# Three tables of places remade: the same 8,797 steps of a graph network kernel in another order of issue

## The chip, the cores and the metric

The kernel runs on one core of a Trainium2 chip. Its metric is device microseconds (us) for one launch. The kernel before took 1741.71 us in the median of three runs (1741.22 to 1742.57).

Five engines work on their own queues, each strictly in the order in which the program issued to it: TensorE (PE, matmuls and transposes), VectorE (DVE), ScalarE (ACT), GpSimd (POOL) and SyncE (SP, which here only issues DMAs). An instruction that needs another engine's result waits at the head of its own queue, and all that stands behind it waits too.

## What is computed

Sixteen independent graphs of 1024 nodes with 256 features go through two layers. `adj` holds 0 or 1 here, so of the first layer's four edge kinds only the first occurs.

```python
# layer 0: gate every edge by the nodes' own product
e     = leaky(einsum('bid,bjd->bij', x * a0, x))         # slope 0.2
alpha = sigmoid(where(adj == 1, e, -max))
x     = layernorm(x + einsum('bij,bjd->bid', alpha, x) + bias)
# layer 1: attention with four heads of 64 features
Wh    = (x @ W).reshape(B, N, H, F)
e     = leaky_relu(e_src[:, :, None, :] + e_dst[:, None, :, :], 0.2)
alpha = softmax(where(A > 0, e, -1e9), axis=2)
Hout  = elu(einsum('bijh,bjhf->bihf', alpha, Wh))
x     = layernorm(x + Hout.reshape(B, N, H * F))
```

The softmax is not evaluated edge by edge. Each exponential is a product of a factor of the source and one of the target, with one of two slopes. So the kernel only decides for each edge which slope holds (`pos`, a 0/1 matrix), multiplies that matrix by the targets' factors (`acc`), multiplies the whole mask by the same factors (`total`), and joins the two sums afterwards.

## The kernel before, in words

`stages` (line 194) writes one graph's work as some fifty Python generators, one for each stage. Every `yield` ends a **step**: one instruction, or a few of one kind. `issue` (line 1229) decides the order in which all steps of all graphs are issued. It takes a table of **places** for each graph: `FIRST` (line 1008) for graph 0, `LAST` (line 1120) for graph 15, `TIMES` (line 902) for those between. A table has a number for each step of each stage; graph b's numbers are shifted by b times `PERIOD` (112.0), everything is sorted by number, and the steps are issued in that order. Equal numbers keep the order of the table. The numbers are written like microseconds, but nothing waits for a clock: only the order counts, and no scheduler changes it afterwards (`manual_schedule`). Semaphores hold each instruction until its inputs are there, whatever the order.

Three graphs are always under way at once, so the queue of each engine is a weave of three graphs' stages. In the order of one graph, with the engine and the line of its instruction:

- loads of `adj` (aload, SP, L267) and of x (xload, SP, L253); `cast` to bf16 (ACT, L276); `turn`, a transpose of the mask by DMA (SP, L291; in graph 0 on PE, L286); `mask` (ACT, L298).
- `xt`, `xtc`, `xta`: x transposed and scaled (PE L319, ACT L330, ACT L344).
- `score` (PE, L356, 12 steps), `leak` (ACT, L368) and `leaky` (DVE, L376), `sigmoid` (ACT, L382). Only the upper triangle is computed; `below` (PE, L395) and `lower` (DVE, L401) mirror it, `upper` (DVE, L412) masks it, `self_loop` (DVE, L419) adds the identity.
- `agg` (PE, L427, 16 steps), then `residual` (DVE, L459), `moments0` and `gathered0` (DVE, L444 and L450), `spread0` (POOL, L468 and L469), `shift0` (DVE, L477), `norm0` (ACT, L489): the first layer's end.
- `yt`, `ytc`, `project`, `wh` (PE L498, ACT L507, PE L517, ACT L529). `sources`, `rows`, `keep_rows` (ACT L535, PE L541, ACT L552 and a DMA at L553) put one row per head and block into DRAM; `sload` (SP, L648) reads a row back, spread over all partitions.
- `top_dve` (DVE, from L560) and `top_pe` (PE, L588 and L591), `exps` (ACT, L598): the factors. `product` (DVE, L619; half of them on ACT, L614, in graph 15), `high` (ACT, L633) and `low` (DVE, L640) split them into two parts in `gm`, of which there is one buffer for all graphs.
- `pos` (DVE, L658, 64 steps) and `acc` (PE, L670, 64 steps of four matmuls): for each half of the nodes and each head, eight steps. `acc_low` (ACT, L685) and `acc_sum` (DVE, L693) empty the sums. There are six `pos` buffers and two accumulators.
- `all_edges` (ACT, L705, 16 steps) and `total` (PE, L713, 32 steps of four matmuls), `total_kept`, `total_less`.
- `weigh`, `divide`, `elu`, `join` (DVE L780, L772, L790 to L810; ACT L816; in graphs 14 and 15 the wide products go to ACT, L767), `moments1`, `gathered1`, `spread1`, `shift1`, `norm1`, and `leave` (SP, L876) sends a half of the graph out. `weigh_end` to `join_end` work on the last head of graph 15 alone.

Four PSUM banks (`ps_t`) are shared by `xt`, `score`, `below`, `agg`, `yt`, `project`, `rows`, `top_pe` and `total`: the next of these waits until the fourth before it has been read. The order of issue so also sets the order in which the banks go round, and what a bank waits for.

Of the kernel before, what the change touches and what calls it, by code (L numbers as in the profile page):

```python
# [193 lines left out]
def stages(nc, k, pl, b, xg, adjg, outg, sums, span, zinv):  # L194
# [675 lines left out]
    def leave():  # L870
# [32 lines left out]
    "xload": [-190.36],  # L903
    "aload": [-141.21, -134.94, -129.14, -126.41, -107.72, -95.92, -52.91, -49.35],
    "cast": [-133.33, -126.54, -110.85, -106.42, -72.33, -55.28, -40.89, -29.41],
    "turn": [-133.00, -118.97, -108.09, -86.35, -62.89, -45.14, -38.49, -26.07],
    "mask": [-126.25, -118.09, -94.06, -70.56, -52.12, -40.03, -32.69, -25.15],
    "setup": [-54.43, -50.76, -47.38],
    "xt": [-69.63, -66.83, -65.59, -61.38],
    "xtc": [-65.35, -64.69, -63.96, -57.76],  # L910
    "xta": [-60.02, -56.47, -53.23, -47.62, -40.80, -39.84, -35.73, -22.45],
    "score": [
        -55.95, -54.26, -52.86, -52.85, -50.30, -47.61, -41.77, -41.05, -37.61, -36.60,
        -31.53, -19.69,
    ],
    "leak": [
        -54.25, -52.28, -52.05, -51.99, -45.24, -41.19, -38.48, -36.59, -34.23, -28.07,
        -26.47, -19.19,
    ],
    "leaky": [  # L920
        -53.92, -51.61, -45.43, -45.41, -41.52, -40.38, -37.19, -36.20, -32.91, -26.88,
        -25.80, -17.05,
    ],
    "sigmoid": [-50.37, -36.56, -28.45, -23.28, -23.17, -15.81, -5.09, 4.38],
    "below": [-43.48, -40.73, -36.17, -28.75, -25.55, -24.80, -21.22, -11.11, 7.22, 7.95],
    "lower": [-41.97, -37.35, -33.23, -27.18, -24.41, -23.38, -19.01, -9.26, 8.37, 17.62],
    "upper": [-24.74, -21.21, -20.88, -18.06, 1.37, 12.57, 17.16, 22.61],
    "self_loop": [-22.52, -20.95, -18.10, -17.88, 3.26, 14.07, 18.13, 24.49],
    "agg": [
        -18.25, -16.27, -15.06, -15.02, -4.11, -4.03, -2.54, 0.32, 5.09, 8.13, 15.85,  # L930
        17.47, 21.46, 23.59, 23.78, 24.56,
    ],
    "residual": [-8.35, -7.46, -1.27, 2.37, 22.46, 22.48, 26.43, 27.74],
    "moments0": [-5.49, -4.53, 5.61, 8.01, 23.75, 25.11, 27.16, 28.13],
    "gathered0": [4.13, 6.42, 7.91, 10.51, 26.40, 27.32, 28.51, 29.05],
    "spread0": [13.40, 31.26],
    "shift0": [17.29, 31.54],
    "norm0": [21.66, 21.89, 22.47, 23.38, 34.53, 34.91, 35.50, 35.54],
    "yt": [27.46, 27.57, 36.68, 36.99],
    "ytc": [29.00, 29.33, 39.29, 39.57],  # L940
    "project": [32.52, 32.60, 33.90, 39.19, 40.28, 40.33, 40.41, 40.81],
    "wh": [33.22, 36.59, 37.58, 40.10, 40.68, 42.17, 42.34, 43.12],
    "sources": [41.16, 45.78],
    "rows": [41.83, 54.07],
    "keep_rows": [44.82, 56.53],
    "top_dve": [43.38, 45.01, 45.39, 50.81, 51.81],
    "top_pe": [44.42, 46.92],
    "exps": [51.81],
    "product": [53.02, 53.37, 53.98, 54.66, 58.34, 66.43, 69.20, 72.08],
    "high": [53.76, 54.40, 58.33, 58.56, 61.32, 68.49, 71.81, 73.63],  # L950
    "low": [54.19, 57.97, 61.74, 62.89, 71.04, 72.63, 75.29, 76.96],
    "sload": [50.80, 79.07, 83.92, 88.62, 102.34, 116.17, 128.36, 142.07],
    "pos": [
        57.31, 58.08, 60.13, 63.67, 69.85, 70.05, 71.57, 77.68, 80.69, 81.39, 82.09,
        82.79, 83.51, 84.84, 85.08, 85.50, 94.75, 97.25, 97.29, 97.48, 99.31, 100.22,
        100.86, 101.86, 104.39, 105.08, 105.66, 107.42, 108.55, 108.94, 109.06, 109.44,
        111.06, 112.18, 112.18, 112.50, 114.43, 114.99, 117.57, 118.23, 118.61, 122.99,
        125.51, 126.22, 128.00, 128.98, 130.58, 132.32, 133.80, 134.68, 135.40, 135.59,
        136.35, 141.70, 144.45, 144.66, 145.90, 146.60, 148.13, 149.39, 151.16, 153.05,
        156.93, 159.83,  # L960
    ],
    "acc": [
        66.06, 67.27, 68.14, 69.24, 71.32, 72.44, 73.71, 78.80, 83.16, 83.97, 84.72,
        85.39, 85.74, 87.50, 88.94, 90.52, 99.28, 99.52, 100.60, 101.24, 101.47, 101.85,
        102.15, 102.38, 108.43, 108.66, 109.45, 109.46, 109.72, 110.12, 110.70, 110.77,
        114.66, 115.11, 115.34, 116.25, 116.73, 118.20, 118.35, 119.33, 130.24, 130.46,
        130.54, 131.53, 132.09, 132.57, 134.85, 134.91, 141.46, 142.49, 142.93, 144.35,
        145.14, 145.81, 145.91, 146.87, 153.97, 154.83, 159.23, 159.59, 164.73, 165.20,
        165.32, 166.33,
    ],  # L970
    "acc_low": [
        79.49, 79.83, 96.76, 97.23, 103.47, 104.76, 112.24, 112.31, 122.02, 122.21,
        134.93, 135.59, 149.34, 149.98, 169.77, 170.85,
    ],
    "acc_sum": [
        80.66, 80.96, 97.10, 98.04, 105.15, 105.96, 112.53, 112.54, 127.47, 127.48,
        136.59, 136.70, 149.39, 150.00, 171.97, 175.58,
    ],
    "all_edges": [
        24.35, 76.79, 79.33, 79.88, 81.06, 82.66, 85.63, 89.08, 96.83, 101.38, 102.99,  # L980
        108.02, 111.52, 113.15, 116.96, 118.15,
    ],
    "total": [
        77.14, 77.24, 78.75, 79.22, 79.40, 79.41, 79.97, 80.39, 84.60, 84.83, 85.08,
        85.73, 89.40, 89.80, 90.91, 93.34, 97.93, 100.95, 101.71, 106.58, 107.02, 107.21,
        109.68, 110.76, 112.06, 113.36, 114.66, 114.68, 117.04, 118.18, 118.28, 119.92,
    ],
    "total_kept": [80.79, 83.22, 90.91, 93.71],
    "total_less": [112.64, 113.12, 119.31, 124.40],
    "weigh": [119.49, 129.29, 190.71, 191.25, 196.08, 212.23],  # L990
    "divide": [
        125.16, 126.39, 127.60, 129.50, 130.49, 134.23, 134.70, 134.85, 200.68, 201.14,
        206.69, 213.74, 214.56, 214.57, 216.22, 218.60,
    ],
    "elu": [133.27, 142.72, 214.93, 220.17],
    "join": [136.57, 142.87, 142.93, 145.63, 220.24, 222.78, 225.82, 228.23],
    "moments1": [146.58, 148.42, 152.65, 153.15, 223.48, 227.82, 229.78, 230.58],
    "gathered1": [146.81, 150.62, 154.63, 154.74, 228.81, 229.65, 230.64, 230.81],
    "spread1": [164.98, 232.04],
    "shift1": [165.77, 237.22],  # L1000
    "norm1": [195.74, 197.90, 202.92, 203.03, 238.05, 240.07, 240.16, 240.29],
    "leave": [206.44, 240.93],
    "weigh_end": [222.86, 228.40],
    "divide_end": [222.94, 223.01, 223.09, 223.17, 228.57, 228.75, 228.92, 229.09],
    "elu_end": [223.25, 229.26],
    "join_end": [223.32, 223.40, 229.44, 229.61],
}
FIRST = {
    "aload": [-146.50, -146.40, -145.60, -145.40, -145.20, -144.50],
    "cast": [-146.00, -145.00, -144.10, -143.30, -142.40, -141.30, -140.80, -140.10],  # L1010
    "turn": [-145.50, -144.80, -144.00, -143.00, -141.90, -140.90, -140.30, -139.30],
    "mask": [-145.10, -144.30, -142.70, -142.60, -141.20, -140.50, -139.70, -139.00],
    "setup": [-145.90, -142.90, -140.70],
    "xt": [-147.40, -147.20, -146.90, -146.80],
    "xtc": [-147.10, -146.70, -146.30, -146.10],
    "xta": [-146.60, -145.70, -144.70, -143.40, -141.50, -140.90, -139.60, -138.50],
    "score": [
        -146.20, -144.90, -144.40, -143.70, -143.10, -142.30, -142.00, -141.80, -140.40,
        -139.10, -138.80, -137.70,
    ],  # L1020
    "leak": [
        -145.80, -144.60, -143.90, -143.50, -142.80, -142.20, -141.40, -140.60, -140.00,
        -138.40, -138.10, -137.30,
    ],
    "leaky": [
        -145.30, -144.20, -143.60, -143.20, -142.50, -141.70, -141.00, -140.20, -139.40,
        -138.30, -137.60, -137.20,
    ],
    "sigmoid": [-143.80, -142.10, -138.70, -137.80, -136.80, -136.70, -135.00, -134.80],
    "below": [  # L1030
        -141.60, -140.00, -139.80, -139.30, -138.20, -137.10, -136.90, -136.60, -135.50,
        -134.60,
    ],
    "lower": [
        -141.10, -139.90, -139.50, -139.20, -137.00, -136.50, -136.40, -135.70, -134.90,
        -132.90,
    ],
    "upper": [-138.90, -138.00, -136.30, -136.10, -135.20, -134.30, -134.20, -133.50],
    "self_loop": [-138.60, -137.50, -135.90, -135.40, -134.40, -133.30, -133.10, -131.70],
    "agg": [  # L1040
        -137.90, -137.40, -136.20, -136.00, -135.80, -135.30, -134.50, -133.80, -133.60,
        -133.20, -133.00, -132.50, -132.20, -132.10, -131.90, -131.00,
    ],
# [434 lines left out]
```

## Time and profile before

| what | value |
|---|---|
| median of three runs | 1741.71 us |
| span of the profiled execution, first to last instruction | 1739.6 us |
| mean granted TensorE clock | 0.990 |
| busy: PE, DVE, ACT, POOL | 97%, 94%, 71%, 6% |
| first steady stretch to last: PE busy from 200 to 1600 us | 1399.4 of 1400 us |
| PE busy, 0 to 80 us and 1650 to 1740 us | 69.7 of 80 us and 54.7 of 90 us |
| DVE busy, 0 to 80 us and 1650 to 1740 us | 35.8 of 80 us and 80.3 of 90 us |
| time from one graph to the next in the steady stretch | 104.44 us |

The profiled execution's span ends some 2.1 us short of the runs' median; the rest lies ahead of its first instruction and behind its last one. A busy share counts the time in which an engine has at least one instruction under way. Matmuls overlap: a matmul of `agg` is shown as 379 ns long, but the next one starts 216 ns after it. So a busy share of PE says that PE had something under way, and what a row costs is read from start to start.

### The profile page before, as it was taken

The numbers are of one execution on the slowest core, as the hardware profiler recorded it, in microseconds if no ns is written. First come the engines' busy times: TensorE is split into PE (matmuls) and PEld (weight loads), VectorE is DVE, ScalarE is ACT, GpSimd is POOL, SyncE is SP. The second block draws the span as 40 slices with busy tenths as digits, with TensorE's granted clock in tenths as the row PEclk, the third lists the DMA queues.
The fourth block names the chain that finished last, engine by engine and source line by source line (L and its number), as shares of the span: only waits on it lengthen the run. The fifth ranks groups of instructions, "written<-read, shape, count | busy, mean of one in ns | idle before, by whom it ended". The sixth has DMA issues, their size and how long they took to land.

```text
span 1739.6 us, 29647 instructions
## 1 busy us (share of the span) xinstructions
PE 1692.1 (97%) x10580; PEld 1492.5 (86%) x10580; DVE 1639.6 (94%) x3663; ACT 1239.4 (71%) x2766; POOL 106.8 (6%) x138
## 2 busy tenths in 40 slices
PE   8999999999999999999999999999999999999984
PEld 5789898998979889898998979889898898979883
DVE  5498999999999999999999999999999999999998
ACT  7674957759587685967759587685967859586784
POOL 0000000010000101000010000101000010000100
PEclk9999999999999999999999999999999999999987
DMA  5542333434334343333435334443343424422020
GB/s 190 129 116 67 98 98 92 110 92 131 88 89 101 105 125 92 94 101 92 109 92 129 91 86 102 105 128 91 89 107 92 110 67 117 105 71 55 26 68 26
DMA packets 249005, 168.59 MB, mean 97 GB/s; under 512 B 133010, under 2 KB 232468, under 8 KB 248852
## 3 DMA queue, kind: packets, MB, share of 16 engines
q1 hardware_dynamic: 248848, 166.63, 36.1%
q8 instruction: 86, 1.41, 0.3%
q14 instruction: 67, 0.55, 0.1%
q10 hardware_dynamic: 4, 0.00, 0.0%
HBM read 118.10 MB, written 17.04 MB: 78 GB/s over the span
## 4 chain that ended last, share of the span: by engine, by line
PE 91%; DVE 3%; ACT 2%; DMA 1%; issue 1%; POOL 0%; SPq 0%; ACTq 0%; DVEq 0%; POOLq 0%
PE acc L670 27%; PE agg L427 24%; PE tot L713 14%; PE e L356 13%; PE pw L517 7%; PE pg L395 3%; PE pt L498 2%; PE pt L319 1%; DVE pos L658 1%; DMA sbc<-sdram 1%; ACT prod L614 0%; DMA aT<-a 0%; PE pbc L591 0%; ACT gm L633 0%; ACT y L489 0%
## 5 line engine op out<-in xcount | busy, mean ns | idle before, releaser
L658 DVE SCALAR_TENSOR_TENSOR pos<-sbc,nd,mT 128x512 fp32r<-128x512 f32 x1024 | 737.4, 745 | 10.5 <-PE acc L670 5.0
L670 PE MATMUL acc<-gm,pos 128*128 128x260 f32 x4096 | 608.6, 292 | 8.9 <-DVE gm L640 5.0
L670 PEld LDWEIGHTS acc<-gm,pos 128*128 128x128 f32 x4096 | 536.8, 190 | 19.8 <-issue 5.7
L427 PE MATMUL agg<-xb,gate 128*128 128x256 f32 x2048 | 463.5, 379 | 0.2
L427 PEld LDWEIGHTS agg<-xb,gate 128*128 128x128 f32 x2048 | 379.9, 190 | 47.6 <-DVE gate L419 1.2
L713 PE MATMUL tot<-gm,allm 128*128 128x264 f32 x2048 | 328.8, 297 | 5.4 <-ACT gm L633 4.9
L713 PEld LDWEIGHTS tot<-gm,allm 128*128 128x128 f32 x2048 | 281.4, 189 | 9.7 <-ACT gm L633 5.1
L356 PE MATMUL e<-xT,xTa 128*128 128x512 f32 (+3 forms) x768 | 264.3, 489 | 2.2 <-ACT xTa L344 1.4
L356 PEld LDWEIGHTS e<-xT,xTa 128*128 128x128 f32 x768 | 135.1, 191 | 106.4 <-issue 55.3
L685 ACT COPY low<-acc 128x260 f32<-128x260 f32 x256 | 89.8, 377 | 187.5 <-PE acc L670 187.3
L705 ACT CAST allm<-mT 128x512 fp32r<-128x512 uint8 x256 | 157.4, 615 | 33.4 <-PE tot L713 31.7
L489 ACT ACTIVATE y<-y,shift,rstd 128x256 f32<-128x256 f32 x254 | 136.3, 592 | 48.6 <-DVE shift L477 48.6
L276 ACT ACTIVATE a<-a 128x1024 bf16<-128x1024 int32 x124 | 131.3, 1059 | 32.1 <-DMA aT<-a 23.0
L298 ACT ACTIVATE mT<-aT 128x1024 uint8<-128x1024 bf16 x120 | 127.1, 1059 | 7.6 <-DMA aT<-a 7.5
L468 POOL TENSOR_SCALAR std<-mv 128x4 f32<-128x4 f32 x64 | 27.7, 432 | 1618.7 <-DVE mv L450 1447.1
L517 PE MATMUL pw<-w_aug,yT 128*128 128x264 f32 x512 | 121.8, 387 | 0.5 <-ACT yT L507 0.5
L376 DVE TENSOR_TENSOR gate<-e,gate 128x512 f32<-128x512 f32 x192 | 105.5, 556 | 14.5 <-ACT gate L368 14.4
L693 DVE TENSOR_TENSOR u<-acc,low 128x260 f32<-128x260 f32 x256 | 103.1, 425 | 10.5 <-ACT low L685 10.3
L444 DVE BATCH_NORM_STATS2 st<-y 128x6 f32<-128x256 f32 x256 | 107.5, 421 | 1.2
L517 PEld LDWEIGHTS pw<-w_aug,yT 128*128 128x128 f32 x512 | 93.4, 190 | 15.4 <-ACT yT L507 1.9
L368 ACT ACTIVATE gate<-e 128x512 f32<-128x512 f32 x192 | 90.2, 486 | 13.7 <-PE e L356 13.3
L412 DVE TENSOR_TENSOR gate<-gate,mT 128x1024 f32<-128x1024 f32 (+7 forms) x128 | 96.6, 755 | 2.9 <-ACT mT L298 2.4
(111 smaller groups left out, 1788.8 us busy)
## 6 DMA issues: line engine op xcount, KB each, us to landing
a<-in_adj_dram SPq DMA_DIRECT2D x124, 512.0 KB, 4.6
sbc<-sdram SPq DMA_DIRECT2D x128, 256.0 KB, 4.6
out_dram<-y SPq DMA_DIRECT2D x31, 512.0 KB, 3.5
xb<-in_x_dram SPq DMA_DIRECT2D x15, 1024.0 KB, 5.4
a_us<-in_adj_dram SPq DMA_DIRECT2D x4, 512.0 KB, 8.9
aT<-a SPq DMA_TRANSPOSE x120, 3.1
xb<-in_x_dram SPq DMA_DIRECT2D x2, 512.0 KB, 4.7
sdram<-srow SPq DMA_DIRECT2D x32, 8.0 KB, 1.4
```

What stands on the lines that cost most here:

```text
L276: nc.scalar.activation(t["a16", ib], t["a32", ib], AF.Copy, accum_out=sums[:, 0, at : at + 1])
L298: nc.scalar.activation(t["mT"][:, :, ib * P : (ib + 1) * P], t["aT", ib], AF.Square, accum_out=sums[:, 1, at : at + 1],)
L356: nc.tensor.matmul(e[:, 0:n], lhsT=t["xTa", jb][:, c, :], rhs=t["xT"][:, c, at : at + n], start=(c == 0), stop=(c == DC - 1),)
L376: nc.vector.tensor_tensor(ge, t["e", jb, at][:, 0:n], ge, ALU.max)
L427: nc.tensor.matmul(agg[:, 0:D], lhsT=t["gate"][:, jb, ib * P : (ib + 1) * P], rhs=t["xb"][:, jb, :], start=(jb == 0), stop=(jb == NB - 1),)
L444: nc.vector.bn_stats(st, t["y", half][:, q, :])
L489: nc.scalar.activation(y, y, AF.Identity, bias=shift, scale=rstd)
L517: nc.tensor.matmul(pw[:, 0:WD], lhsT=t["yT"][:, c, jb * P : (jb + 1) * P], rhs=k.w_aug[:, c, :], start=(c == 0), stop=(c == DC - 1),)
L658: nc.vector.scalar_tensor_tensor(p_, t["sbc", half, h], t["nd"][:, jb, h : h + 1], t["mT"][:, jb, half * HALF : (half + 1) * HALF], ALU.is ...
L670: nc.tensor.matmul(t["acc", half, h, q // 2][:, q % 2, 0 : 2 * E], lhsT=t["pos", half, h, jb][:, q * P : (q + 1) * P], rhs=pl.gm[:, h, jb] ...
L705: nc.scalar.copy(m_, t["mT"][:, j0 : j0 + 4, ib * P : (ib + 1) * P])
L713: nc.tensor.matmul(tot[:, 0 : H * F1], lhsT=t["allm", ib, jb // 4 * 4][:, jb % 4, :], rhs=pl.gm[:, :, jb, l, F:E], start=(jb == 0 and l == 0),
```

## The change

Every number in `TIMES`, `FIRST` and `LAST` is replaced; `PERIOD` stays. The stages, their instructions, the tiles and the buffer counts are the same. On PE 8,899 matmuls, on DVE 3,663 instructions and on ACT 1,336 activations and 1,087 copies are issued before and after; ACT loads its function tables 89 times where it was 87. A few entries of the diff:

```diff
 TIMES = {
-    "score": [-55.95, -54.26, -52.86, -52.85, -50.30, -47.61, ...],
+    "score": [-57.69, -54.01, -54.01, -50.95, -50.68, -45.88, ...],
...
 FIRST = {
...
 LAST = {
-    "keep_rows": [39.35, 108.12],
+    "keep_rows": [44.86, 100.53],
-    "shift1": [5876.75, 6450.18],
+    "shift1": [5913.40, 6450.78],
-    "norm1": [5887.78, 5934.77, 5954.41, 6153.71, 6461.98, 6650.47, 6748.07, 6844.90],
+    "norm1": [5920.27, 5920.27, 5968.24, 6113.98, 6705.61, 6705.61, 6705.61, 6832.23],
```

What the order becomes is seen in the queues. Four places, each written as stage and step number, with +1 for the next graph and -1 for the one before:

```
SP, graph 0      before  keep_rows[0]  turn+1[4]  sload[0]  keep_rows[1]  ...  turn+1[6]  sload[1]
                 after   keep_rows[0]  sload[0]  aload+1[5]  turn+1[4]  ...  keep_rows[1]  turn+1[5]  aload+1[6]  sload[1]
PE, graph 0      before  yt[2-3] project[4-7] xt+1[0] rows[0] xt+1[1] top_pe[0]
                 after   yt[2-3] project[4] rows[0] project[5-7] xt+1[0-1] top_pe[0]
PE, each graph   before  score[0-5] acc-1[0-2] below[0] acc-1[3] score[6-7] below[1] acc-1[4-6] score[8-9] below[2] total-1[0-2] acc-1[7] total-1[3-7]
                 after   score[3-5] acc-1[0-2] score[6-7] acc-1[3-5] below[0] score[8] acc-1[6] score[9] total-1[0-2] below[1] acc-1[7] total-1[3-5] score[10] total-1[6-7]
DVE, graph 15    before  ... divide_end[7] shift1[0] moments1[4] join[6] ... gathered1[6-7] shift1[1]
                 after   ... join[7] gathered1[5] moments1[6-7] gathered1[6-7] shift1[0-1]
```

## The prediction

> **What bounds the kernel now.** I read the page first: its opening line, the busy line and the shares of the chain that ended last.
>
> ```profile
> span 1739.6 us, 29647 instructions
> PE 1692.1 (97%) x10580; PEld 1492.5 (86%) x10580; DVE 1639.6 (94%) x3663; ACT 1239.4 (71%) x2766; POOL 106.8 (6%) x138
> PE 91%; DVE 3%; ACT 2%; DMA 1%; issue 1%; POOL 0%; SPq 0%; ACTq 0%; DVEq 0%; POOLq 0%
> ```
>
> The chain runs along PE for 91% of the span, so PE sets the end, but DVE is close behind. Busy times by stretch (time, then PE, PEld, DVE, ACT, POOL with counts, granted clock, DMA) tell the two regimes apart:
>
> ```profile
> 700.00:800.00 100.00, 100.00 (x630) 88.49 (x629) 97.79 (x219) 71.58 (x155) 6.60 (x8) 1.00 0.39 106
> 1650.00:1700.00 50.00, 40.09 (x291) 39.30 (x292) 49.03 (x99) 38.92 (x123) 1.69 (x2) 0.86 0.20 59
> ```
>
> In the middle PE is never idle and DVE has 2.2% spare. From 1645 us (the last graph has no successor to feed PE) it is the other way round: DVE 98%, PE 80%. Third, the chain between two graphs (start, us, what):
>
> ```profile
> 709.78 9.02 PE e L356 x24
> ...
> 757.54 3.45 PE agg L427 x16
> 760.99 1.92 PE acc L670 x16
> ```
>
> The same piece of `e` starts again at 814.24, so a graph takes 104.46 us. How much of that is matmul? Start to start, such rows give 0.120 us for an `acc` (1.92 / 16), 0.216 for an `agg` (3.45 / 16), 0.126 for a `total` and 0.223 for a projection. A graph has 256, 128, 128 and 32 of these: 30.7 + 27.6 + 16.2 + 7.1. Scores add 15.5, transposes and mirrors (60 at 0.109) 6.5, small ones 0.6: 104.2 us. So only some 0.25 us of a graph is PE waiting, and no order can win more than that in the steady stretch: 13 x 0.25 = 3.3 us of 1740. What else order can move lies in the head (until about 104 us) and in the tail.
>
> **The change part by part.** Nothing is added or removed: the matmul, DVE and activation counts are equal, and the two more table loads (1.28 us each) fall on ACT, which is 28% idle in the steady stretch: nothing, and 2.6 us if they fell where ACT is late. What moves is the place of each step.
>
> *Head.* Up to the first `agg` at 35.87 us ACT works without a gap from 11.5 on, and what it must finish before the last mask is the same in both orders: nothing. Then the `agg`s run gapless to 65.3. After it, the chain before reads:
>
> ```profile
> 76.04 0.26 ACT srow L552
> ...
> 76.32 0.34 SPq L553
> ...
> 76.71 1.24 SPq L291
> ...
> 77.99 4.52 DMA sbc<-sdram
> 82.51 0.03 issue
> 82.54 0.75 DVE pos L658
> ...
> 97.11 4.57 DMA sbc<-sdram
> 101.68 0.03 issue
> 101.71 0.75 DVE pos L658
> ...
> 103.20 1.10 PE e L356 x4
> ```
>
> The row of a source goes out (L553), a mask transpose of the next graph (`turn+1[4]`, L291) stands between on SP's queue, then the row is read back and `pos` starts. The new order issues `sload[0]` right after `keep_rows[0]`, and `rows[0]` after `project[4]` instead of after `project[7]` and a transpose. The transpose on SP (1.24) and three projections' worth of PE work (some 1.5 to 2 us) leave the path: the read-back lands near 79.7 instead of 82.5. The whole 2.8 us is not won, for the factors are late next: `exps` ended at 79.17 and has one ACT copy (0.59) less ahead of it, so 78.6, and the products and `low[0]` on DVE follow. I get `pos[1]` at 82.76 instead of 83.81, 1.05 us earlier. The second read-back (97.11) made DVE idle 1.24 us before 101.71; it waits for a buffer that `pos[7]` frees, and `pos[7]` stands six places earlier in DVE's new queue, so that wait goes. Against these stand four more DVE instructions that follow their own input (0.12 each, see below), and a bank that `below+1[2]` has to empty. Sum at the first `total` after 104 us: **-1.3**, bounds 0 (the factors cover it all) and -2.5 (both waits gone in full).
>
> *Steady stretch.* PE has at most 0.25 to give. In the new order the mirrors (`below`) stand further behind their scores and the `total`s closer together; both ease the waits of PE a little. I take 0.1 of the 0.25: 13 x -0.1 = **-1.3**, bounds 0 and -3.3 while PE stays the bound. But DVE pays. Two rows of its timeline show what a neighbour costs: the first pair waits for its own predecessor, the second does not.
>
> ```profile
> 65.92 0.43 DVE L444 BATCH_NORM_STATS2 st<-y 128x6 f32<-128x256 f32 x1
> 66.38 0.18 DVE L450 BATCH_NORM_AGGREGATE mv<-st 128x2 f32<-128x6 f32 x1
> ```
>
> ```profile
> 596.94 0.17 DVE L450 BATCH_NORM_AGGREGATE mv<-st 128x2 f32<-128x6 f32 x1
> 597.03 0.72 DVE L658 SCALAR_TENSOR_TENSOR pos<-sbc,nd,mT 128x512 fp32r<-128x512 f32 x1
> ```
>
> The dependent one starts 0.03 us after its predecessor's end, the independent one 0.08 before it: 0.12 us apart. Of such pairs the built queues hold 143 before and 256 after, 8 and 16 for a steady graph. DVE's work for a graph goes from 97.79% of 104.45 = 102.1 to 102.1 + 8 x 0.12 = 103.1; its spare falls from 2.3 to 1.3 us. While PE is the bound this costs nothing; if the cover is gone, see the rival below.
>
> The Trainium skill speaks against this price: "VectorE: DVE Perf Modes", section "The DRAIN you can't avoid", has the pipeline drained at every instruction's end and semaphores added for nothing, eight copies taking 13.88 us with a semaphore after each or only after the last. By it the dependent pairs would cost no more than others, and the tail below would come out 0.5 lower. The rows above show 0.12 between the two kinds of pair, and I go by the rows.
>
> *Tail, from 1645 us.* DVE is the bound, so its sum counts. The last graph has 17 dependent pairs where it had 9: 8 x 0.12 = 0.96, of which 0.5 is left when the shorter overlaps around them are summed row by row: +0.5. Four `acc` of graph 14 (0.12 each) now stand ahead of the last projection: +0.5. The end itself:
>
> ```profile
> 1726.98 2.06 ACT L489 ACTIVATE y<-y,shift,rstd 128x256 f32<-128x256 f32 x4
> ...
> 1729.06 4.21 SPq L876 DMA_DIRECT2D out_dram<-y  x3
> ...
> 1731.56 0.16 DVE L477 SCALAR_TENSOR_TENSOR shift<-mv,rstd 128x4 f32<-128x4 f32 x1 [1.47 <-POOL rstd L469]
> 1731.76 1.09 ACT L489 ACTIVATE y<-y,shift,rstd 128x256 f32<-128x256 f32 x2 [2.72 <-DVE shift L477]
> ```
>
> Before, `shift1[0]` and the first half's norms (2.06 on ACT) are over before the last moments end at 1730.08, and ACT then does two norms only. In the new order `shift1[0]` is issued next to `shift1[1]`, so six norms of 0.55 (1.09 / 2) are left for ACT at the very end, 3.2 us after the last moments instead of 2.8 (the first four start at once, since their `rstd` is long there): +0.4; and the first half's 512 KB go out just ahead of the last quarter, sharing the DMA engines with it: 0 to +0.9. I take +0.65 for the two together. Sum **+1.65**. Bounds: the stalls that DVE had in the tail before are some 3 us (work 71.2 of 74.2 us up to the last sum); all of them gone gives -1, and as much again gives +4.
>
> *Sum.* 1739.6 - 1.3 - 1.3 + 1.65 = 1738.65 for a profiled span; the runs' median lies 2.1 above the span: **1740.7**, or 0.06% less than before. A measurement of this kernel tells about 0.2% (3.5 us) from no change.
>
> **The rivals.**
> *Faster: the waits all go.* If the steady stretch gets its 0.25 back in full (-3.3), the head the whole -2.5 and the tail comes out even, 1741.7 - 5.8 = 1735.9. For it: DVE's waits before (for gates 14.4 us, `low` 10.3, `rstd` 9.0 over the run) come from steps placed too close behind their inputs, and an order can place them better. Against it: PE is at 99.8% already.
>
> *Slower: DVE becomes the bound.* DVE now loses about 2.3 us of every graph to waits on ACT, POOL and PE:
>
> ```profile
> DVE gate L376 <- ACT gate L368: 14.4, 18, 3.2
> ...
> DVE u L693 <- ACT low L685: 10.3, 14, 1.3
> DVE span L560 <- ACT wh L529: 9.4, 3, 7.7
> DVE shift L477 <- POOL rstd L469: 9.0, 17, 1.5
> ```
>
> Part of that is only its spare time, spent waiting. But if the new order keeps them, 103.1 + 2.3 = 105.4 us for a graph beats PE's 104.45: +1.0 for each of 13 graphs, +13, so up to 1754. It decides from where DVE's unavoidable waits pass 1.3 us a graph; at 1.8 the time is 1747. For it: the spare is 1.2%, and 0.12 us a pair is itself a mean. Against it: most of these waits are short and would shrink by themselves when DVE runs later.
>
> *Nothing is changed* is excluded: the built queues differ in all five engines, PE's by some 3,000 lines.
>
> **How the numbers follow.** Forecast (within 3.5 us of 1741.7): 0.52. Faster by the waits, 1734 to 1738: 0.27. DVE as the bound, 1746 to 1754: 0.21. The likeliest case alone spans 1738 to 1745, by the bounds of head and tail. The range leaves out the far end of each rival, about a tenth on either side: 1734 to 1749. Faster by over 0.2% 0.27, within 0.52, slower 0.21.
>
> **What would show it.** Head: the first `sbc` read-back lands near 80 us and no SP transpose stands in the chain; the `total`s after 104 start near 103. Steady: `e` recurs every 104.3 to 104.4 us, PE at 100% and DVE near 98.7% of a 100 us stretch; a period over 104.6 with PE idle and DVE at 99% and more is the slow rival. Tail: DVE from 1645 to the last moments takes about 1 us longer, six norms at the end on ACT, and the last output lands some 3.5 us after the last moments. I am wrong if the head's gain is eaten by the factors, if the dependent pairs cost nothing or twice 0.12, or if a wait that the queues do not show (a PSUM bank, a `pos` buffer) opens in the steady stretch.

## The result and the profile after

The new order takes **1746.76 us** (median of seven runs, 1745.89 to 1748.32) against 1741.71 (seven runs, 1740.99 to 1742.57): ratio 1.0027, interval 1.0016 to 1.0038. It is 5 us slower where 1 us less was forecast. The page of the new kernel, its opening line, its busy line and the shares of the chain that ended last:

```profile
span 1744.1 us, 29481 instructions
PE 1695.3 (97%) x10580; PEld 1492.1 (86%) x10580; DVE 1649.2 (95%) x3663; ACT 1244.3 (71%) x2768; POOL 116.8 (7%) x138
PE 87%; DVE 5%; ACT 4%; issue 2%; DMA 1%; POOL 0%; ACTq 0%; POOLq 0%; DVEq 0%
```

The span is 4.5 us longer, DVE busy 9.6 us more, and the chain goes along DVE and ACT for 9% of the span where it was 5%. PE's share of busy time says nothing. To see where the time went, the same step is looked up in both traces, and its time before is subtracted:

| milestone | before, us | after minus before |
|---|---|---|
| first `agg` of graph 0 | 35.87 | +1.01 |
| first `top_dve` of graph 2 | 285.80 | -1.03 |
| first `top_dve` of graph 14 | 1540.41 | +3.69 |
| first `top_dve` of graph 15 | 1644.96 | +4.43 |
| last `gathered1` of graph 15 | 1730.09 | +3.50 |
| end of the span | 1739.62 | +4.45 |

So in these two profiles the head wins 1.0 us; from graph 2 to graph 14 4.7 us are lost, at the step from graph 14 to graph 15 another 0.7, and behind it nothing. (The 1.0 holds for these two profiles only: PE's clock has a part in it, see the last section.) From graph 6 to graph 9 the time of a graph is 104.77 us where it was 104.45, and twice (graphs 5 and 10) there is a step of 1 us more.

**What a full PE hides.** A stretch of the new kernel by engine (time, then PE, PEld, DVE, ACT, POOL with counts, clock, DMA):

```profile
700.00:1000.00 300.00, 300.00 (x1886) 264.91 (x1885) 294.83 (x647) 223.44 (x485) 20.06 (x22) 1.00 0.40 105
```

PE is busy for all of it, as before (DVE 293.91 then), and still each graph takes 0.33 us more. A matmul's span overlaps the next one's, so a wait of 0.2 us does not show as PE idle. It shows in the distance from start to start, compared with the usual distance of the same two operations. In each steady graph of the new kernel one place stands out: a transpose of `yt` (L498) starts 0.27 us after the one before it and not 0.11, and the one after it 0.06 late: 0.22 us. A smaller one, 0.09 us, is at the second matmul of `agg[0]`; together they make the 0.33, nearly. The timeline at the transpose:

```profile
801.58 1.59 ACT L489 ACTIVATE y<-y,shift,rstd 128x256 f32<-128x256 f32 x3 [2.17 <-DVE shift L477]
803.07 0.35 ACT L529 COPY wh<-pw 128x264 f32<-128x264 f32 x1
803.33 0.60 ACT L489 ACTIVATE y<-y,shift,rstd 128x256 f32<-128x256 f32 x1
803.98 0.53 PEld L498 LDWEIGHTS pt<-ident,y 128*128 128x128 f32 x5 [0.24 <-ACT y L489]
```

The four norms before `yt` started when `shift0` came from DVE, and the copy `wh[1]` stands between the third and the fourth; PE waits for the fourth, and the row of the weights (PEld) has the wait that the row of the matmuls hides.

The steps of 1 us are another wait. At 533 us:

```profile
530.27 1.06 ACT L298 ACTIVATE mT<-aT 128x1024 uint8<-128x1024 bf16 x1 [0.88 <-DMA aT<-a]
...
532.37 1.08 ACT L489 ACTIVATE y<-y,shift,rstd 128x256 f32<-128x256 f32 x2
533.36 0.35 ACT L749 COPY ts<-tot 128x264 f32<-128x264 f32 x1
...
533.76 0.92 PE L427 MATMUL agg<-xb,gate 128*128 128x256 f32 x3 [0.81 <-ACT ts L749]
```

`agg[0]` needs the bank that `ts` (`total_kept[2]`) empties. That copy stands behind a mask, a cast and two norms on ACT. The mask's transpose landed 6.2 us after its issue here and 6.1 at the second step; in most other graphs it took 4.4 to 4.8 (before: mostly 3.1). The steps come and go with such landings: in `first_old` below three took 6.1 to 6.3 us and there are three steps, in `pairs_apart` one took 6.2 (the other 4.7) and there is one. Why just these land late stays open.

### The profile page after: what moved, and what is told of

Read it like the earlier page. It is cut to its first block, busy times and chain, and to the rows that moved or that the text cites. A ratio compares the mean times of both kernels' runs of the same rounds, so it can differ in the third digit from the quotient of the medians.

```text
span 1744.1 us, 29481 instructions
## 1 busy us (share of the span) xinstructions
PE 1695.3 (97%) x10580; PEld 1492.1 (86%) x10580; DVE 1649.2 (95%) x3663; ACT 1244.3 (71%) x2768; POOL 116.8 (7%) x138
## 4 chain that ended last, share of the span: by engine, by line
PE 87%; DVE 5%; ACT 4%; issue 2%; DMA 1%; POOL 0%; ACTq 0%; POOLq 0%; DVEq 0%
PE acc L670 25%; PE agg L427 24%; PE e L356 13%; PE tot L713 13%; PE pw L517 6%; PE pg L395 2%; DVE pos L658 2%; PE pt L319 2%; PE pt L498 2%; DMA aT<-a 1%; ACT mT L298 0%; ACT a L276 0%; ACT u L767 0%; ACT prod L614 0%; ACT gm L633 0%
## 5 line engine op out<-in xcount | busy, mean ns | idle before, releaser
L658 DVE SCALAR_TENSOR_TENSOR pos<-sbc,nd,mT 128x512 fp32r<-128x512 f32 x1024 | 725.9, 747 | 6.2 <-PE acc L670 6.1
L713 PE MATMUL tot<-gm,allm 128*128 128x264 f32 x2048 | 321.9, 297 | 0.8 <-ACT allm L705 0.8
L356 PE MATMUL e<-xT,xTa 128*128 128x512 f32 (+3 forms) x768 | 270.8, 490 | 1.7 <-ACT xTa L344 1.2
L489 ACT ACTIVATE y<-y,shift,rstd 128x256 f32<-128x256 f32 x254 | 139.8, 593 | 99.6 <-DVE shift L477 97.7
L468 POOL TENSOR_SCALAR std<-mv 128x4 f32<-128x4 f32 x64 | 33.5, 524 | 1612.4 <-DVE mv L450 1350.0
L507 ACT COPY yT<-pt 128x512 f32<-128x512 f32 x64 | 34.5, 589 | 85.3 <-PE pt L498 85.2
```

Source lines behind the costliest of these rows:

```text
L356: nc.tensor.matmul(e[:, 0:n], lhsT=t["xTa", jb][:, c, :], rhs=t["xT"][:, c, at : at + n], start=(c == 0), stop=(c == DC - 1),)
L489: nc.scalar.activation(y, y, AF.Identity, bias=shift, scale=rstd)
L658: nc.vector.scalar_tensor_tensor(p_, t["sbc", half, h], t["nd"][:, jb, h : h + 1], t["mT"][:, jb, half * HALF : (half + 1) * HALF], ALU.is ...
L713: nc.tensor.matmul(tot[:, 0 : H * F1], lhsT=t["allm", ib, jb // 4 * 4][:, jb % 4, :], rhs=pl.gm[:, :, jb, l, F:E], start=(jb == 0 and l == 0),
```

## The experiments

DVE's time is split thus: where more than 50 ns pass between the end of an instruction and the start of the next, the excess over 34 ns (the usual distance of a dependent pair) is a wait; the rest is its work. Work and waits so add up to the time of a graph by definition. A shorter wait counts as work: in the new kernel and in `yt_fix` one `pos` of each graph starts 0.01 to 0.02 us after its predecessor's end and not 0.08 ahead of it as in `ts_fix`, 0.1 us of "work" that is a wait. Averages of graphs 6 to 8:

| kernel | one graph, us | DVE's work | DVE's waits |
|---|---|---|---|
| before | 104.45 | 102.78 | 1.66 |
| after | 104.77 | 103.70 | 1.07 |
| `yt_fix` | 104.55 | 103.70 | 0.85 |
| `ts_fix` | 104.66 | 103.59 | 1.07 |
| `tail_fix` | 104.45 | 103.57 | 0.87 |
| `all_fix` | 104.46 | 103.59 | 0.87 |
| `pairs_apart` | 104.55 | 102.13 | 2.42 |
| `all_pairs` | 104.45 | 102.14 | 2.31 |
| `dve_more_before` | 105.06 | 103.99 | 1.07 |
| `dve_more_after` | 106.12 | 104.96 | 1.16 |

**One table at a time.** `first_new` is the kernel before with the new `FIRST`; `first_old` is the new kernel with the old `FIRST`.

> The kernel before with the new order of graph 0 alone. Theory (the new order loses in the steady stretch, and the head is a gain): agg[0] of graph 0 about 1 us later than before, because the last cast of graph 0 waits for a transpose of its predecessor behind the mirrors on PE, but the gap closes and top_dve[0] of graph 2 comes 0.5 to 1.5 us earlier than before; after that the period stays 104.45 us and the whole run ends 0.5 to 1.5 us earlier: 1740.2 to 1741.2 us. Rival (the new head is what costs): the run ends 1 us or more later than before, 1742.7 us or more.

> The new kernel with the old order of graph 0: the new orders of the steady stretch and of the last graph alone. Theory: agg[0] of graph 0 at 35.9 us as before; a period of 104.77 us; 1 to 2 us longer than the whole change, 1747.5 to 1749 us. Rival (the head costs): 1743 to 1745 us, shorter than the whole change.

Measured: 1772.58 and 1767.61 us (ratios 1.0177, 1.0164 to 1.0191, and 1.0147, 1.0132 to 1.0163). Both expectations on the time missed: graphs 0 to 2 of one table do not fit graphs 1 to 3 of the other, and the first 330 us lose 20 to 30 us. So the head's worth can't be had this way; `first_new` meets its first rival's number but not for its reason, since the whole change holds the same head. What the two do show is the steady stretch: from graph 6 to 9 a graph takes 104.44 us in `first_new` and 104.77 in `first_old`. The loss belongs to the new `TIMES` and does not come from the head. The new `TIMES` with the old `LAST`, and the new `LAST` with the old `TIMES`, were not run: at the seam of the two orders each would probably wait for the other, as in these two runs. So the tail alone was not tried.

**The norm behind the copy.** `yt_fix`:

```diff
-    "norm0": [..., 35.87, 35.87, 37.92],
+    "norm0": [..., 35.87, 35.87, 36.00],
```

> The new kernel with one place changed: in the table of the steady stretch norm0[7] goes from 37.92 to 36.00, so that ACT runs the last of four norms ahead of the copy wh[1] and not behind it. Theory (PE waits 0.22 us in each graph at yt for that norm): the period falls from 104.77 to 104.55 us, 14 x 0.22 = 3.1 us less: 1743.7 us. Rival (DVE, with more pairs that wait for their own predecessor, sets the period): the wait moves to another place, the period stays above 104.7 and the time within 1 us of 1746.8.

Measured: **1743.43 us**, ratio 1.0009 (0.9999 to 1.0018); a graph 104.55 us. The four norms now stand together, and the copy behind them:

```profile
802.70 2.08 ACT L489 ACTIVATE y<-y,shift,rstd 128x256 f32<-128x256 f32 x4 [2.15 <-DVE shift L477]
803.74 1.05 PE L517 MATMUL pw<-w_aug,yT 128*128 128x264 f32 x4
```

One place of 8,797, issued 0.26 us (the copy) earlier in each graph, gives back 3.3 of the 5 us. What a graph still takes above 104.45 us is the 0.09 at `agg[0]`, unchanged here.

**The copy behind two norms.** `ts_fix`:

```diff
-    "total_kept": [79.48, 82.72, 92.96, 98.08],
+    "total_kept": [79.48, 82.72, 92.40, 98.08],
```

> The new kernel with one place changed: total_kept[2] goes from 92.96 to 92.40, so that ACT empties the bank that agg[0] waits for ahead of two norms (1.08 us) and not behind them. Theory (a late mask transpose pushes that copy past the moment when PE needs the bank, 1 us each time, in two graphs of the profile): no step of 1 us between agg[0] of neighbouring graphs, 2 us less than the new kernel: 1744.8 us, and a smaller spread between runs; the 0.22 us at yt stays and the period is 104.77. Rival: the steps come from elsewhere (a queue of DMAs, DVE) and stay; 1746.8 us.

Measured: **1744.69 us**, ratio 1.0016 (1.0007 to 1.0025), and no step of 1 us is left: the waits at `agg` from graph 2 to 14 fall from 2.97 to 0.07 us, some 1.1 turn up at a score ahead of it, so the same two graphs still take 0.6 us more than the others (105.23 and 105.26 us). The spread between runs did not shrink (1742.58 to 1746.28). Not expected: a graph takes 104.66 us, 0.11 less. In every graph the 0.09 at the second matmul of `agg[0]` is gone as well: the late copy cost a little each time, and much in two graphs.

**The pairs.** `yt_fix` alone can't say why the norm was late. `pairs_apart` leaves ACT's order as it is and moves twelve DVE steps by a few neighbours (`moments0`, `gathered0`, `divide`, `join`, `gathered1`), so that of 16 dependent pairs 3 are left:

```diff
-    "moments0": [-10.49, -2.59, -0.04, 3.32, 27.04, 29.05, 31.70, 33.41],
-    "gathered0": [-10.46, -1.99, 5.23, 5.40, 27.30, 32.60, 33.18, 34.26],
+    "moments0": [-10.49, -2.30, -0.04, 3.32, 27.04, 29.75, 31.70, 33.41],
+    "gathered0": [-8.80, -1.99, 5.23, 5.40, 28.73, 32.60, 33.18, 34.26],
```

> The new kernel with twelve places of the steady table changed, all of DVE steps, each by a few neighbours: of the 16 DVE pairs of a steady graph in which an instruction waits for the one just before it, 3 are left (8 in the kernel before). The two fixes of ACT's order are not in it. Theory (the 8 added pairs lengthened DVE's work for a graph by 0.9 us, and DVE with its recurring waits of 1.1 to 1.2 us sets the period of 104.77): DVE's work falls by 13 x 0.12 = 1.56 us for a graph, the period falls to PE's own 104.45 to 104.5, the wait of PE at yt shrinks from 0.22 to under 0.05 us although the copy still stands ahead of the norm; 13 x 0.3 = 3.9 us less, 1742.9 us (the two steps of 1 us stay). Rival (the place of the copy alone makes the wait at yt, the pairs are covered by DVE's idle time): period still 104.7 or more, 1746 us or more.

Measured: 1744.07 us, ratio 1.0011 (1.0002 to 1.0020). The mechanism is as stated: DVE's work falls by 1.57 us for a graph (1.56 were expected), a graph takes 104.55 us, and the wait at `yt` is gone though the copy still stands there; the 0.09 at `agg[0]` stays, as in `yt_fix`. The run moves places as well as parting pairs; what DVE's work does by itself is tried below. The run's time missed by 1.2 us, and the milestones tell where: up to graph 14 it gains 3.7 us on the new kernel (0.9 of it because the second step of 1 us did not come), but the step from graph 14 to 15 takes 107.13 us, 1.8 more than in the new kernel. `all_pairs` is this and all fixes below together:

> The run all_fix (two places of ACT, turn[6], shift1[0]) and the twelve places of pairs_apart together. Theory: both cure the same lateness, so no sum of gains: the period can't fall below PE's 104.45 us; 0 to 0.5 us below all_fix, 1739.9 to 1740.4 us. Rival (DVE still sets the period in all_fix, whose DVE work is 103.59 and waits 0.87 us a graph): the period falls well below 104.46, 2 us or more less than all_fix.

Measured: 1743.21 us, ratio 1.0005 (0.9996 to 1.0014), 2.8 us more than `all_fix` (2.1 by the ratios) and than its forecast; a graph takes 104.45 us, PE's own time, so the gains do not add, as expected. The step from graph 14 to 15 takes 107.14 us (`all_fix` 105.29); the rest is about what the two starts of PE differ by (last section). DVE's waits of `all_pairs` from 1600 to 1652 us name what holds it:

```profile
DVE u L790 <- ACT u L767: 3.1, 1, 3.1
```

In graph 14 the wide products are on ACT; the `divide` steps that I moved wait for them there, 3.1 us where it was 0.5.

**How much DVE has to spare.** In `dve_more_before` and `dve_more_after` two `pos` of each graph from 1 to 14 are written twice:

```diff
-                nc.vector.scalar_tensor_tensor(
+                for _ in range(2 if (h, jb) == (2, 4) and 0 < b < k.B - 1 else 1):
+                    nc.vector.scalar_tensor_tensor(
```

> The kernel before with two pos of each of graphs 1 to 14 written twice (the second write repeats the first): 2 x (0.66 to 0.78) = 1.3 to 1.6 us more DVE work for each graph. Theory (PE sets the period, DVE has some 2 us spare): the period rises by less than 0.3 us, the run by 0 to 4 us. Rival (DVE is as good as the bound, its waits are not spare): the period rises by 1.0 us or more, the run by 14 us or more.

> The new kernel with two pos of each of graphs 1 to 14 written twice: 1.3 to 1.6 us more DVE work for each graph. Theory (PE sets the period here too; DVE's busy share is 98.2% and not 97.8%, so it has 0.4 us less spare than before, not 1.0): the period rises by 0 to 0.5 us, the run by 0 to 7 us. Rival (the pairs that wait for their own predecessor have taken the spare, so that DVE is the bound): the period rises by the whole 1.3 to 1.6 us, the run by 18 us or more.

Measured: 1750.93 us (ratio 1.0049, 1.0034 to 1.0065) and 1765.90 us (1.0132, 1.0116 to 1.0147). With some 1.25 us more work a graph takes 0.61 us longer before and 1.35 us longer after. So both theories of mine fall: before, DVE had some 0.6 us to spare and not 2; after, none at all, and there the rival held (18 us or more; 19.1 measured). The stretch from 700 to 1000 us in `dve_more_after`, and the wait of PE's weights for the norms from 640 to 1060 us (in all, times, longest), which has grown with DVE's work:

```profile
700.00:1000.00 300.00, 298.20 (x1860) 261.35 (x1859) 294.52 (x644) 220.93 (x481) 21.69 (x22) 1.00 0.39 100
```

```profile
PEld pt L498 <- ACT y L489: 4.7, 12, 0.6
```

DVE is no busier than in the new kernel (98.2%), though it is the bound: the 1.1 us of waits come back in every graph. The two largest are these, in the new kernel from 640 to 1060 us:

```profile
DVE span L560 <- ACT wh L529: 1.8, 4, 0.4
DVE shift L477 <- POOL rstd L469: 1.1, 4, 0.3
```

The first is the end of a loop: DVE's moments give `shift0`, ACT's norms follow, PE's `yt` and projections wait for them, ACT's `wh` for those, and DVE's `top_dve` for `wh`. Nothing in it can be filled by other work, since DVE's order is fixed.

**The end and the head.** `tail_fix` has the two ACT places of above and `shift1[0]` of graph 15 at 5881.80, not 5913.40. `all_fix` has in addition `turn[6]` of graph 0 at -139.40, not -136.21.

> The new kernel with three places changed: norm0[7] at 36.00 and total_kept[2] at 92.40 in the steady table, and in the table of the last graph shift1[0] at 5881.80 and not at 5913.40, so that four of the six norms at the end run before the last moments. Theory: 3.1 us from the first, 2 us from the second, and at the end the last landing comes 5.2 us after the last moments (as before) and not 6.65: 0.9 us. 1746.8 - 6.0 = 1740.8 us. Rival (the first two gains overlap, since both waits are PE slack of the same kind, and the end is set by the flag's chain and not by the outputs): 1742.5 us or more, and the span's end stays 10.4 us after the last moments.

> As the run tail_fix, and in the table of graph 0 turn[6] at -139.40 and not at -136.21, so that PE transposes that block ahead of two mirrors and ACT's last cast of graph 0 doesn't wait for it (1.24 us). Theory: agg[0] of graph 0 at 35.7 us, 1.2 us earlier than in the new kernel, and the run 0.5 to 1.2 us shorter than tail_fix: 1739.7 to 1740.3 us, a little below the kernel before. Rival (what follows the agg runs sets the pace: the read-backs and the factors): agg[0] earlier, but top_dve[0] of graph 2 and the end unchanged, within 0.3 us of tail_fix.

Measured: **1741.25 us** (ratio 0.9994, 0.9985 to 1.0003) and **1740.40 us** (0.9993, 0.9984 to 1.0002). Both forecasts of the time held within 0.5 us, and the two ACT places together bring a graph back to 104.45 us. The reasons held less well. In the new kernel the end reads:

```profile
1733.51 0.13 DVE L477 SCALAR_TENSOR_TENSOR shift<-mv,rstd 128x4 f32<-128x4 f32 x1
1733.67 3.06 ACT L489 ACTIVATE y<-y,shift,rstd 128x256 f32<-128x256 f32 x6 [3.38 <-DVE shift L477]
```

Six norms at the end, and the last output lands 6.65 us after the last moments (before: 5.21). In `tail_fix` it lands 5.23 after them, but the span ends 10.24 us after them, not 9.5 as before (the new kernel: 10.48). The end hangs on the flag that all engines read, 4.02 us after the last moments in each of these kernels, and on a branch of PE behind it, which takes 3.6 us before, 3.8 in the new kernel and 4.3 to 4.4 in the fixed ones. So the rival had the end right: 0.2 us came of it, not 0.9. Why PE's branch differs stays open; in `ts_fix`, whose end is the new kernel's, it takes 4.6.

The head's fix moved the wait: ACT's cast no longer waits for the transpose on PE, but a mask now waits 1.1 us for another one. Of the 1.2 us expected at `agg[0]` only 0.24 came (35.53 in `tail_fix`, 35.29 in `all_fix`). The rest of what seems a gain on the new kernel is the start of PE, which differs between runs of the same instructions (last section). `all_fix` beats the new kernel by 6 us; from the kernel before its interval does not tell it apart.

## Why the prediction was wrong

1. **What bounds the kernel.** Right in the bound: in the kernel before added work of DVE costs only half of itself. The 0.25 us of PE's waits was not tested; the fixed kernels also come to 104.45 and not below. The mistake is beside it: "DVE has 2.2% spare", 2.3 us of a graph, was read from the busy share. `dve_more_before` puts the spare at 0.6 us.
2. **The head, -1.3.** Measured -1.03 at graph 2, but this is partly luck. The read-back landed at 80.46 us (79.7 forecast), `pos[1]` started at 83.61 (82.76), and the wait before the second read-back went. But "what it must finish before the last mask is the same in both orders: nothing" failed: ACT's instructions are the same, and yet the last cast waits 1.2 us for a transpose that PE does behind scores and mirrors, in a stretch in which the new head has PE at half its clock (last section); the prediction has no term for that. `agg[0]` came 1.01 us later, so from there the order won 2 us and not 1.3. At graph 2 the kernels with this head and about as slow a start of PE stand at -1.07, -1.03 and -0.86, but `yt_fix`, where the clock drops a second time at 81.6 us, at +0.87. With a quick start on both sides the new head loses: the first `top_dve` of graph 1 starts at 181.17 us in `tail_fix` (which has that second drop too) and at 179.00 in `dve_more_before`, with a slow start at 180.50 (new kernel) and 180.69 (before). So the sign of the head's gain is not settled. The new kernel's chain has no read-back and no SP in it any more, the scores of graph 1 run on from the factors:

```profile
80.35 0.31 ACT xTa L344
80.66 0.04 issue
80.71 8.42 PE e L356 x20
```

3. **The steady stretch, -1.3. This is the step that failed**: +4.7 from graph 2 to graph 14. Twelve graphs at 0.33 are 3.9, the two steps 1.9, and the kernel before lost 1.1 to steps of its own, which the new one doesn't have. Two terms were missed. First, "while PE is the bound this costs nothing": the price of the pairs was about right (8 x 0.12 = 0.96; DVE's work rose by 0.92, of which 0.1 is the short wait named above the table), but the cover was not 2.3 us. With work added, DVE's waits stay at 1.07 and 1.16 us a graph. That is my own slower rival, which "decides from where DVE's unavoidable waits pass 1.3 us a graph". Its mechanism was right, its sizes were not: the 1.3 stood on a work of 103.1 us read from the busy share, where the split gives 103.70, so 1.07 us of waits were enough; and as I let it keep all of the old waits, it had +1.0 a graph (1747 at the least, with a chance of 0.21), where the wait at `yt` is 0.22. By `yt_fix` and `pairs_apart` either a shorter path from DVE to PE or another order of DVE with less work ends it. Second, the late copy `ts` costs 0.09 us in each graph and 1 us in two, behind a late mask. The prediction has no term for it; it is the wait on a PSUM bank that stood among its signs of being wrong.
4. **The tail, +1.65.** Measured +0.74 at the step from graph 14 to 15 and +0.02 behind it. The four `acc` ahead of the last projection (+0.5) are the 0.74, as far as the queues show: they take 0.67 us there, and that step is 105.29 us in all six kernels that have the new `TIMES` and `LAST` and no change of DVE's steady steps (before 104.55). The end cost +0.95 (0.65 taken, bounds 0.4 to 1.3): right in size, but by another way. Neither the norms nor the last landing set the end. All of it lies behind the flag: its load takes 1.1 us while the outputs go out and 0.7 in the kernel before and in `tail_fix`; PE's branch adds 0.2, and DVE is done 0.3 us after PE. The dependent pairs (+0.5) were wrong: from the first `top_dve` of graph 15 to the last moments DVE's work rose by 0.02 us, and its waits fell from 1.32 to 0.37. I had counted them as unchanged.
5. **The sum.** The range reached to 1749 because of that rival, and the time lies in it; but the sign was wrong, and the likeliest case's own end, 1745, was passed. That 1746.76 is close to the rival's 1747 is luck: 0.22 a graph, the rival's own part, makes 2.6 us in the twelve graphs, and the copy `ts` 3.0.

Of the Trainium skill's rule that a semaphore adds nothing to the drain ("VectorE: DVE Perf Modes", "The DRAIN you can't avoid"): the runs decide for the rows: 13 pairs less are worth 1.57 us in `pairs_apart` and 1.45 from `all_fix` to `all_pairs`, 0.11 to 0.12 each. The same section also says that a next instruction which is not held starts earlier, which the prediction left out; the rows of independent pairs, 0.08 us ahead of the predecessor's end, agree with that.

## What to carry to other kernels

Idle time of an engine is spare only where something else can fill it: add a known amount of work to it and see how much the time grows, before a cost is put down as covered. Where two engines are both over 97% busy, look for the loop that goes through both, and price the change by the work of the second engine plus the waits that come back each time round. An in-order queue makes single places dear: one copy of 0.26 us ahead of a norm was worth 3 us here, and the wait stood in the row of the weights, not in that of the matmuls. And before a gain of 1 us is put down to an order, compare the granted clock of the two profiles.

## What the hardware showed besides

PE starts at one of several paces. The first four passes of `e` of graph 0, the same instructions, in the new kernel and in `all_fix`:

```profile
8.31 3.03 PE L356 MATMUL e<-xT,xTa 128*128 128x512 f32 x4
```

```profile
7.94 1.88 PE L356 MATMUL e<-xT,xTa 128*128 128x512 f32 x4
```

The granted clock reads 1.00 for both in the views, but the trace's records of it begin only at 10.6 us in the new kernel and at 7.6 us in `all_fix`; ahead of that there is none. The passes follow these records: 0.85 us from start to start ahead of them, 0.43 behind. Where the start is slow, `agg[0]` comes 1.3 us or so later (`all_pairs` 36.56, `all_fix` 35.29, with one and the same head; the new kernel 36.88, `tail_fix` 35.53), so a head can be compared only between runs with the same start. The Trainium skill ("TensorE: Matmul & The Clock Gate", "Part 1: The HAM clock gate (the "warmup" mystery)") has a cause that fits: PE runs at half speed for about its first 3.4 us of work, and the window that decides it runs free, so that the moment differs from run to run. Here the change comes 2.7 us (`all_fix`) to 5.8 us (new kernel) after PE's transposes begin at 4.8 us.

The clock also drops later. In every kernel with the new `FIRST` it is 0.50 for 3.4 us, in the new kernel from 27.7 to 31.1 us, and in no kernel with the old one does it drop there. The first 40 us, before and after (the clock is the third number from the end):

```profile
0.00:40.00 40.00, 32.01 (x164) 20.28 (x165) 20.03 (x50) 30.01 (x58) 1.26 (x10) 1.00 0.59 201
0.00:40.00 40.00, 31.58 (x157) 20.82 (x158) 19.69 (x51) 28.76 (x53) 1.26 (x10) 0.96 0.57 201
```

Some 2 us ahead of the drop PE waits 2.39 us for a cast; in the kernel before its longest wait in that part is 1.08. In the drop four passes of `e` take 2.88 us that take 1.94 at full clock, and the mirrors behind them are slowed too. So 0.9 us or more of the last cast's wait is the clock's, as an estimate from these rows; no run has this head without the drop. A second drop of 3.4 us begins at 79 to 82 us in `yt_fix`, `tail_fix`, `all_fix`, `all_pairs` and `dve_more_after`, and is missing in the new kernel, `ts_fix` and `pairs_apart`. Up to there the order of `yt_fix` is the new kernel's, and yet twenty passes of `e` take 10.12 us in it and 8.42 in the new kernel. How many of the unprofiled runs had this drop is not on record.

The traces show when the clock drops. Its records begin and end on a grid of 3.41 us, which starts with the first record, 10.6 us in the new kernel and 9.9 in `yt_fix`. Cut into pieces on this grid, the twelve traces have 59 drops, each behind a piece at full clock in which PE was busy for at most 0.574 of the time; only three pieces as empty as that have no drop behind them, of some 5,900 without one. In `yt_fix` the piece from 78.2 us is filled to 0.574, in the new kernel the one from 78.9 us to 0.66: the same work, cut elsewhere. Whether the head loses that 1.7 us hangs on where the grid lies, and that differs between runs.

Last, a transpose by DMA that landed in 3.1 us at most places took 4.4 to 6.2 at another place of the queue.
